# One core, gated cross-attention and feed-forward products: a frozen order of operations in place of a list planned at build time

## The chip, the cores and the metric

The kernel runs on one core of a Trainium2 chip. The metric is the device time of one execution in microseconds (us); the median of several runs is compared. One execution of each kernel was also recorded by the hardware profiler, and "the profile", "the trace" and "the timeline" below are views of that one execution.

## The reference, cut to what matters

```python
def fake_quant(x, scale, zp):
    q = jnp.clip(jnp.round(x / scale + zp), 0.0, 255.0)
    return (q - zp) * scale

x = x + tanh(g_xattn) * (fake_quant(layernorm(x)) @ fake_quant(ctx_4096))     # (2,1024,2048) @ (2,2048,2048)
x_ei = concat([layernorm(x)[..., :1638], -4.0 * layernorm(x)[..., 1638:]])
x = x + tanh(g_ffn) * scale * einsum('bsi,if->bsf', x_ei, kernel)            # kernel: 2048 x 2048, boolean
```

Both products have 2048 rows of tokens (two batches of 1024), an inner length of 2048 and 2048 output columns. The first product works on whole numbers from 0 to 255, the second on 32-bit floats against a matrix of zeros and ones.

## The kernel before

**Stages.** Tokens are cut into 16 tiles of 128 rows, eight for each batch; two tiles make a pair, and two pairs a quarter `q`. For batch 0 the order is: normalise and quantise the x tiles (`ops_norm1`), quantise the context columns chunk by chunk (`ops_kv`, four chunks `c` of 512 columns, eight loads `g` of 512 KB each), multiply (`mm1`, line 544), add the result to x (`add_row1`, `add_out1`, lines 592 and 596, both on POOL), take the second statistics (`stats`, line 426), scale (`scale2`, line 685), turn by TensorE (`turn2`, line 692), split into a high and a low part (`part_hi`, line 738, ACT; `part_lo`, line 742, DVE or POOL), and multiply with the weights widened from bytes (`widen`, line 782, ACT; `mm2`, line 809). The second product is done for pairs of tiles as seven half-size products `M1` to `M7` with sums of blocks (`combine`, lines 722 to 728, DVE or POOL; `combine_w` for the weights, line 767, DVE); results are added by `add2` (line 825, DVE) onto rows that `load_back` fetched. Batch 1 follows; half of its first product is done in seven products too (`mm1s`, line 646).

**The start.** `load_x` and `load_kv` (lines 420 and 518) are all issued by SP's one queue. `fill_kv` (line 522) is a POOL memset that clears a page before quantised context bytes are written into it. A tile's `stats` (DVE), `variance` (DVE, lines 431 and 433), `square_root` (ACT, line 438) and `factor` (DVE, eight small instructions from line 447) come before its `quant1` (ACT line 470 or DVE line 472), `turn1` (TensorE, line 503) and `take1` (ACT line 512 or DVE line 514). `quant_kv` (ACT line 530 or DVE line 532) quantises one load of context. `sums_mm` (line 556) are TensorE's column sums of the first context chunks, two matmuls for each call; `sums_pair` (lines 565 and 568) prepare those of later chunks on DVE; `row1` (ACT, line 578) takes the column sum. `rowsum1` (ACT line 478, or DVE line 480) sums a token's bytes, and `out1` (ACT line 586 or DVE line 588) takes a product out of PSUM.

**Who sets the order.** Every step is recorded by `op(engines, f, ...)` with the engines that may do it, its reads, writes and buffers. `Plan.order` then plays the recorded steps through a table of durations and waits written in the kernel, 80 times with shifted due times, and returns the best list found, with an engine for every step that has a choice. The list is walked once, and each step emits its instructions:

```python
for o in order:
    if len(o.engines) > 1:
        o.f(*o.args, engine=o.engine)
    else:
        o.f(*o.args)
```

The place of a step in the list therefore fixes three things: its place in its engine's queue (each engine works strictly in order), which of the 44 pages or of the PSUM buffers it gets, and whose release that buffer waits for. A DMA also waits for the landing of the eighth DMA ahead of it.

Of the kernel before, what the change touches and what calls it, by code (L numbers as in the profile page):

```python
# [20 lines left out]
P = 128  # L21
# [5 lines left out]
PAGES = 44  # L27


class Op:  # L30
    __slots__ = ("engines", "f", "args", "deps", "users", "due", "lead", "opens", "uses",
                 "place", "end", "left", "index", "engine", "bias", "port", "ready")


class Plan:

    def __init__(self, buffers):
        self.free = dict(buffers)
        self.ops = []
        self.place = 0.0
        self.writer = {}  # L50
        self.readers = {}
        self.opener = {}
        self.kind = {}
        self.count = {}
        self.first = None

    def op(self, engines, f, *args, reads=(), writes=(), opens=(), main=False, due=None, lead=80, bias=0.0,
           port=False, in_turn=False):

        o = Op()
        o.engines, o.f, o.args, o.lead, o.index = engines, f, args, lead, len(self.ops)
        o.deps, o.users, o.uses, o.opens = set(), [], set(), []
        o.place, o.ready = None, 0.0
        o.due, o.bias, o.port = due, bias, port
        for kind, buf in opens:
            assert buf not in self.opener, buf
            self.opener[buf], self.kind[buf], self.count[buf] = o, kind, 0
            o.opens.append(buf)  # L70
        for key in reads:
            if key in self.writer:
                o.deps.add(self.writer[key])
            self.readers.setdefault(key, []).append(o)
            o.uses.add(key[0])
        for key in writes:
            if key in self.writer:
                o.deps.add(self.writer[key])
            o.deps.update(self.readers.pop(key, ()))
            self.writer[key] = o  # L80
            o.uses.add(key[0])
        for buf in o.uses:
            if buf in self.opener:
                o.deps.add(self.opener[buf])
                self.count[buf] += 1
        if in_turn:
            if self.first is not None:
                o.deps.add(self.first)
            self.first = o
        o.deps.discard(o)  # L90
        for d in o.deps:
            d.users.append(o)
        if main:
            o.place = self.place
            self.place += min(engines.values())
            o.due = o.place if due is None else due
        self.ops.append(o)
        return o

    def dues(self):  # L100
        inf = float("inf")
        given = [o.due for o in self.ops]
        for o in reversed(self.ops):
            d = inf if o.due is None else o.due
            for u in o.users:
                if u.place is not None or u.due is not None and u.due < inf:
                    d = min(d, (u.due if u.place is None else u.place) - min(o.engines.values()) - 3)
            o.due = d
        for o, g in zip(self.ops, given):
            if o.due == inf:  # L110
                o.due = max([d.due for d in o.deps] + [0.0]) + 50

    def order(self, lag, start, runs, seed=1):


        self.dues()
        chance = random.Random(seed)
        free, count = dict(self.free), dict(self.count)
        dues = [o.due for o in self.ops]
        best = None  # L120
        for i in range(runs):
            self.free, self.count = dict(free), dict(count)
            try:
                end = self.run(lag, start)
            except RuntimeError:
                end = None
            if end is not None and (best is None or end <= best[0]):
                best = end, self.began, [o.engine for _, _, o in self.began]
                dues = [o.due for o in self.ops]
                held = self.held_up()  # L130
            for o, due in zip(self.ops, dues):
                o.due = due
            for ops in held:
                if chance.random() < 0.5:
                    step = chance.choice((3.0, 6.0, 12.0, 24.0))
                    for o in ops:
                        o.due -= step
            if i % 3:
                place = chance.uniform(0.0, self.place)
                for o in self.ops:  # L140
                    if o.place is None and abs(o.due - place) < 120.0 and chance.random() < 0.1:
                        o.due += chance.uniform(-25.0, 25.0)
        _, self.began, engines = best
        for (_, _, o), e in zip(self.began, engines):
            o.engine = e
        return [o for _, _, o in self.began]

    def held_up(self):

        before, begin, all_ = {}, {}, []  # L150
        for s, _, o in self.began:
            begin[o] = s
            last = before.get(o.engine)
            before[o.engine], before[o] = o, last
            if o.place is None or last is None or s - begin[last] - last.engines["PE"] < 1.0:
                continue
            ops = []
            x = o
            for _ in range(8):
                x = self.rel.get(x)  # L160
                if x is None or x.place is not None:
                    break
                ops.append(x)
                p = before.get(x)
                if p is not None and begin[p] + p.engines[p.engine] > x.ready + 1.0:
                    break
            all_.append(ops)
        return all_

    def run(self, lag, start):  # L170


        self.rel = {}
        ready = {}
        events = []
        began = []
        for o in self.ops:
            o.left = len(o.deps)
            o.end = 0.0
        tick = 0  # L180

        def push(time, what, o):
            nonlocal tick
            tick += 1
            heappush(events, (time, tick, what, o))

        for o in self.ops:
            if not o.left:
                for e in o.engines:
                    push(0.0, "ready", (e, o))  # L190
        done = set()
        engines = sorted({e for o in self.ops for e in o.engines}, key=lambda e: (e != "PE", e))
        for e in engines:
            ready[e] = []
        busy = {e: e in start for e in engines}
        for e, time in start.items():
            push(time, "idle", e)
        port = 0.0
        progress = 0.0
        now = 0.0  # L200
        idle = 0.0
        last_pe = 0.0
        while len(began) < len(self.ops):
            if not events:
                self.began = began
                raise RuntimeError("the plan is stuck")
            now, _, what, o = heappop(events)
            if what == "ready":
                e, o = o
                if o not in done:  # L210
                    heappush(ready[e], (o.due + o.bias, o.index, o))
            elif what == "idle":
                busy[o] = False
            else:
                for buf in o.uses:
                    if buf in self.count:
                        self.count[buf] -= 1
                        if not self.count[buf]:
                            self.free[self.kind[buf]] += 1
                for u in o.users:  # L220
                    u.left -= 1
                    u.end = max(u.end, now)
                    if not u.left:
                        self.rel[u], u.ready = o, now
                        for e in u.engines:
                            wait = 0.0 if e == o.engine and e != "SP" else lag.get((o.engine, e), lag[e])
                            push(now + wait, "ready", (e, u))
            if events and events[0][0] <= now:
                continue
            again = True  # L230
            while again:
                again = False
                for e in engines:
                    if busy[e]:
                        continue
                    held = []
                    found = None
                    while ready[e]:
# [991 lines left out]
```

## Time and profile before

| what | value |
|---|---|
| median of 3 runs | 698.88 us (698.78 to 699.11) |
| the profiled execution: span, first to last instruction | 697.0 us |
| TensorE (PE): busy, matmuls | 674.0 us, 3180 |
| DVE, ACT, POOL: busy | 490.2, 455.4, 316.8 us |
| first matmul starts | 13.23 us |
| last matmul instruction starts | 692.2 us |
| granted TensorE clock, mean | 1.000 |

The profiled execution has no time of its own beside its span: the page gives 697.0 us, and the median of the timed runs lies 1.9 us above it. In the profile's rows, an arrow `out<-in` names the tiles that an instruction writes and reads; "idle before" is the time for which the engine did nothing just ahead of an instruction, with what ended it.

### The profile page before, as it was taken

To read this page: it belongs to the slowest core of one execution; us is meant where nothing else is said; L and a number is where in the kernel's file an instruction comes from. 1 tells how busy PE (TensorE), PEld (TensorE's weight loads), DVE (VectorE), ACT (ScalarE), POOL (GpSimd) and SP (SyncE) were. 2 spreads that over 40 slices of the span, in tenths; PEclk is the share of its full clock that TensorE was granted. 3 is DMA by queue.
4 is the path that set the end of the run, shared out by engine and by line. 5 is a ranking of instruction groups with operands and counts; after the bars stand their busy time and mean duration, and the time that the engine had idled before them with its cause. 6 is when DMAs were issued, how large, how long until landed. Compare 5 with 4: busy or idle time off the path is not lost.

```text
span 697.0 us, 8833 instructions
## 1 busy us (share of the span) xinstructions
PE 674.0 (97%) x3180; PEld 471.7 (68%) x3180; DVE 490.2 (70%) x717; ACT 455.4 (65%) x536; POOL 316.8 (45%) x210
## 2 busy tenths in 40 slices
PE   1999999989999999999999999999999999999997
PEld 0444444468788888878885444447888888888885
DVE  6899958899998886497878888468572425583331
ACT  4599444286888566699926768229699347689540
POOL 8166789863625221855717887975120101040000
PEclk9999999999999999999999999999999999999999
DMA  8999406777995799477379677327074379155032
GB/s 302 393 393 380 162 13 231 259 261 251 361 400 225 233 324 339 140 247 278 120 263 330 222 268 245 121 92 275 27 260 162 105 231 324 67 170 222 22 131 90
DMA packets 63580, 155.78 MB, mean 223 GB/s; under 512 B 4912, under 2 KB 21296, under 8 KB 63536
## 3 DMA queue, kind: packets, MB, share of 16 engines
q1 hardware_dynamic: 63536, 155.21, 62.9%
q8 instruction: 25, 0.41, 0.2%
q14 instruction: 19, 0.16, 0.1%
HBM read 117.44 MB, written 37.75 MB: 223 GB/s over the span
## 4 chain that ended last, share of the span: by engine, by line
PE 87%; DMA 4%; DVE 4%; POOL 2%; ACT 2%; issue 1%; SPq 0%; ACTq 0%; DVEq 0%
PE acc_M L809 57%; PE acc L544 19%; PE acc_M L646 7%; PE tr L692 4%; DMA kv<-in_kv_dram 3%; DMA x<-in_x_dram 1%; POOL x L596 1%; DVE wB L767 1%; ACT wf_M L782 1%; POOL x L592 1%; PE tr L503 1%; DVE qn L472 0%; PE cs L574 0%; DVE x L685 0%; DVE bn_b L426 0%
## 5 line engine op out<-in xcount | busy, mean ns | idle before, releaser
L809 PE MATMUL acc_M<-wf_M,hi_M 128*128 128x512 f32 x896 | 282.0, 395 | 1.6 <-ACT wf_M L782 1.5
L809 PE MATMUL acc_M<-wf_M,lo_M 128*128 128x512 f32 x896 | 277.6, 390 | 0.6 <-POOL lo_M L742 0.6
L782 ACT ACTIVATE wf_M<-wr_M 128x1024 fp32r<-128x1024 uint8 x224 | 221.6, 1050 | 26.8 <-DMA wr_M<-in_wmask_dram 24.2
L809 PEld LDWEIGHTS acc_M<-wf_M,lo_M 128*128 128x128 f32 x896 | 168.0, 188 | 36.8 <-POOL lo_M L742 1.3
L809 PEld LDWEIGHTS acc_M<-wf_M,hi_M 128*128 128x128 f32 x896 | 164.1, 188 | 34.4 <-ACT wf_M L782 3.2
L544 PE MATMUL acc<-q,q1T 128*128 128x512 f16 x768 | 171.6, 381 | 1.2 <-DVE q1T L514 0.8
L825 DVE SCALAR_TENSOR_TENSOR back<-acc_M,f,back 128x1024 f32<-128x1024 f32 (+1 forms) x58 | 72.1, 1245 | 124.7 <-PE acc_M L809 117.1
L742 POOL TENSOR_TENSOR lo_M<-A,hi_M 128x1024 fp32r<-128x1024 f32 x24 | 62.1, 2586 | 179.5 <-ACT hi_M L738 160.1
L544 PEld LDWEIGHTS <-q1T 128*128 128x128 f16 x768 | 75.2, 98 | 90.2 <-issue 1.9
L592 POOL TENSOR_TENSOR x<-x,row 128x512 f32<-128x512 f32 x64 | 88.6, 1408 | 43.8 <-ACT sd_a L438 15.5
L596 POOL TENSOR_TENSOR x<-x,e 128x512 f32<-128x512 f32 x64 | 92.0, 1458 | 30.6 <-ACT e L586 16.1
L738 ACT CAST hi_M<-A 128x1024 fp32r<-128x1024 f32 x48 | 50.1, 1044 | 13.1 <-POOL A L726 4.7
L530 ACT ACTIVATE q<-kv,sc,rs 128x1024 uint8<-128x1024 f32 x45 | 53.5, 1236 | 7.8 <-DMA kv<-in_kv_dram 5.1
L586 ACT ACTIVATE e<-acc,tokb,f1u 128x512 f32<-128x512 f32 x34 | 25.1, 774 | 49.6 <-PE acc L544 47.8
L426 DVE BATCH_NORM_STATS2 bn_b<-x 128x6 f32<-128x512 f32 x64 | 43.1, 684 | 15.9 <-POOL x L596 15.6
L495 ACT COPY A<-tr 128x512 f32<-128x512 f32 x35 | 20.3, 584 | 46.5 <-PE tr L692 45.8
L742 DVE TENSOR_TENSOR lo_M<-A,hi_M 128x1024 fp32r<-128x1024 f32 x24 | 33.7, 1421 | 7.2 <-ACT hi_M L738 7.2
L568 DVE TENSOR_TENSOR pair<-pair,q 128x1024 f16<-128x1024 f16 x36 | 36.6, 1022 | 2.5 <-ACT q L530 0.8
L728 POOL TENSOR_TENSOR A<-A,A 128x1024 f32<-128x1024 f32 x8 | 21.1, 2648 | 23.7 <-DVE A L726 16.4
L522 POOL MEMSET q<- 128x1024 f32 x32 | 29.2, 952 | 5.1 <-DVE q L532 2.2
L512 ACT ACTIVATE q1T<-tr 128x1024 f16<-128x1024 uint8 x22 | 21.3, 1019 | 7.5 <-PE tr L503 6.8
L767 DVE SCALAR_TENSOR_TENSOR wB<-wB,wB 128x2048 uint16<-128x2048 uint16 x8 | 24.2, 3031 | 0.0
(103 smaller groups left out, 594.1 us busy)
## 6 DMA issues: line engine op xcount, KB each, us to landing
kv<-in_kv_dram SPq DMA_DIRECT2D x64, 512.0 KB, 9.2
x<-in_x_dram SPq DMA_DIRECT2D x32, 512.0 KB, 7.7
x<-x SPq DMA_DIRECT2D x32, 512.0 KB, 3.0
back<-x SPq DMA_DIRECT2D x32, 512.0 KB, 6.1
wr_M<-wt_T SPq DMA_DIRECT2D x32, 512.0 KB, 5.6
out_dram<-back SPq DMA_DIRECT2D x30, 512.0 KB, 3.6
wr_M<-in_wmask_dram SPq DMA_DIRECT2D x24, 512.0 KB, 5.4
n<-in_x_dram SPq DMA_DIRECT2D x16, 512.0 KB, 7.2
```

What stands on the lines that cost most here:

```text
L426: nc.vector.bn_stats(bn[v, t][:, c, :], xt[src[v, t, c // 2]][:, ts(c % 2, NB)])
L530: nc.scalar.activation(low, v, AF.Identity, bias=z2, scale=rs2)
L544: nc.tensor.matmul(acc1[b, c, tiles[0]][:, i, :], q1T[tiles[i]][:, k, :], rhs1(b, c, k), start=(k == 0), stop=(k == KT - 1),)
L568: nc.vector.tensor_add(colsum[b, c], colsum[b, c], v[:, i : i + 2, :])
L592: nc.gpsimd.tensor_add(xc, xc, colrow[b, c])
L596: nc.gpsimd.tensor_add(xc, xc, ev.pop((t, c)))
L646: nc.tensor.matmul(acc1[key][:, i, :], left_half(p, LEFT1[m])[:, 4 * s + k, :], right1(m, h, s)[:, k, :], start=(m in OPENS and s == 0 and ...
L738: nc.scalar.copy(hi[m, p], A[left(m, p)])
L742: engines[engine].tensor_sub(lo[m, p], A[left(m, p)], hi[m, p].bitcast(F32))
L782: nc.scalar.activation(wf[q, m, k], wr[q, m, k // 4][:, k % 4, :], AF.Copy, bias=-float(RIGHT[m][1]))
L809: nc.tensor.matmul(acc2[SUM[m], p][j], part[m, p][:, k, :], wf[q, m, k][:, ts(j, NB)], start=(m in OPENS and k == 0 and part is hi), stop= ...
L825: nc.vector.scalar_tensor_tensor(v, acc, f2, v, ALU.mult, ALU.add)
```

## The change

`Plan` loses its durations, its search and its queue model. `op` still records steps, reads, writes and buffers, and ignores all hints. A string of 2314 words takes the place of the list: a word is a step's number, with D, A or P (DVE, ACT, POOL) where a step has a choice of engine.

```diff
-    order = plan.order({("ACT", "SP"): 8.0, ("POOL", "SP"): 12.0, ("DVE", "SP"): 12.0, "PE": 6.0, ... }, {"SP": 13.0, "DVE": 22.0, "ACT": 22.0}, 80, 2)
-    for o in order:
-        if len(o.engines) > 1:
-            o.f(*o.args, engine=o.engine)
-        else:
-            o.f(*o.args)
+    plan.run(ORDER_OF_OPS)
...
+    def run(self, order):
+        names = {"D": "DVE", "A": "ACT", "P": "POOL"}
+        done = set()
+        for word in order.split():
+            o = self.ops[int(word.rstrip("DAP"))]
+            assert o not in done and o.deps <= done
+            done.add(o)
+            if len(o.engines) > 1:
+                o.f(*o.args, engine=names[word[-1]])
+            else:
+                o.f(*o.args)
+        assert len(done) == len(self.ops)
...
+ORDER_OF_OPS = """
+17 1 137 0 35 38 16 40 95 42 32 48 90 100 37 21 33 20 45 85 5 4 43 84 2 143 3 50 36D 149 6 58 7 19 155 8 213 59
+41A 207 18 9A 47 44D 201 22 94 34A 10D 23 87 229 39A 195 24 11 231 12A 53 233 235 46D 25A 237 89 220 221 13A 26D
...
```

All 2314 steps are the same ones. What differs is their place on each of the five engines, and the engine of 150 of the 342 steps with a choice. The first steps of each queue show the kind of difference (tiles as `load_x(tile, half)`, context as `load_kv(batch, chunk, g)`; `stats(tile, chunk)`):

| queue | before | after |
|---|---|---|
| SP | x(0,0) x(0,1) x(1,0) x(1,1) kv 0,1,2,3,4,5,6,7 | x(1,1) x(0,1) x(0,0) kv 1, x(1,0), kv 3,4,0,2,5, kv(0,1,0), kv 7, x(3,0) x(3,1), kv 6 |
| POOL | 16 fills, in the order of their use | the same 16 fills in another order |
| DVE | stats of tile 0, variance 0, stats(1,0) stats(1,1), factor 0, stats(1,2) stats(1,3), variance 1, quant_kv 1, factor 1 | stats(1,3) (1,2) (0,3) (0,2) (0,0) (0,1), quant_kv 1, variance 0, stats(1,1), factor 0, stats(1,0), quant_kv 4, variance 1, quant1(0,1), factor 1 |
| ACT | sqrt 0, quant_kv 0, quant1(0,0), quant1(0,1), sqrt 1, quant_kv 2, 3, take1(0,0), take1(0,1) | sqrt 0, quant_kv 3, quant1(0,0), quant_kv 0, sqrt 1, quant_kv 2, take1(0,0), quant1(1,0), take1(0,1) |
| PE | sums_mm, turn1 0, 3 sums_mm, 3 mm1 of tile 0, turn1 1 | sums_mm, turn1 0, 4 sums_mm, 4 mm1 of tile 0, turn1 1 |

Further on, the first `turn2` of the second product stands near the end of chunk 0's product of tiles 6 and 7, in place of the start of chunk 3's. Ahead of the first `mm2` stand seven `widen` (four before), two `part_lo` (one before) and three `combine_w` (five before).

## The prediction

> **What bounds it now.** I read the page's head and slices first, then the list of PE's waits, the chain of waits from 120 to 200 us, and the timelines of the start. The head and the slices:
>
> ```profile
> span 697.0 us, 8833 instructions
> PE 674.0 (97%) x3180; PEld 471.7 (68%) x3180; DVE 490.2 (70%) x717; ACT 455.4 (65%) x536; POOL 316.8 (45%) x210
> ...
> PE   1999999989999999999999999999999999999997
> ```
>
> PE is the bound all the way; only the first slice and one about 145 us are not full. Every matmul stays in the change, so time can come only out of PE's gaps. In PE's list of waits:
>
> ```profile
> PE cs L556 <- ACT q L530: 13.2, 1, 13.2
> PE acc_M L809 <- ACT wf_M L782: 1.5, 2, 1.4
> ```
>
> Only the first wait is large. I took the starts of successive matmuls from the trace: 216 ns apart on lines 544, 556 and 646, 227 ns on 809, 109 ns for transposes; what exceeds this is a gap. All matmuls at these paces, with 0.087 us at each of 49 changes from `turn2` to line 809, are 670.9 us of solid work. The gaps are: 13.2 us to the first matmul; half pace (427 ns) until 21.3 us; 2.4 us between 30 and 45 us; 4.0 us after that (0.73 + 0.11 at 145, 1.53 + 0.11 at 151, 0.32 at 186, 0.57 at 258, 0.19 at 299, 0.46 at 394). The last matmul starts at 692.2, the rest is the last add and store, the same in both lists.
>
> The 2.4 us at 145 to 152 come from DVE, by the chain of waits:
>
> ```profile
> 140.39 1.23 DVE wB L767
> ...
> 146.45 3.30 DVE wB L767
> 149.75 0.74 DVE A L706 x2
> ...
> 151.52 1.06 ACT wf_M L782
> ...
> 152.62 8.50 PE acc_M L809 x36
> ```
>
> Weight sums (`combine_w`) stand between DVE's steps for the first `mm2`. The start is the part that decides; timelines of ACT, DVE, POOL and PE:
>
> ```profile
> 11.94 1.24 ACT L530 ACTIVATE q<-kv,sc,rs 128x1024 uint8<-128x1024 f32 x1 [2.03 <-DMA kv<-in_kv_dram]
> 12.33 3.62 POOL L522 MEMSET q<- 128x1024 f32 x4
> 14.23 2.27 DVE L532 TENSOR_SCALAR q<-kv,rs,sc 128x1024 uint8<-128x1024 f32 x1
> 13.23 1.01 PE L556 MATMUL cs<-q,ones_h 128*128 128x512 f16 x2 [13.23 <-ACT q L530]
> 16.55 2.72 PE L556 MATMUL cs<-q,ones_h 128*128 128x512 f16 x6 [0.36 <-DVE r_a L447]
> ```
>
> `quant_kv` on DVE, 0.81 us at its median, took 2.27: it was asked for inside the 15th fill (over at 15.06) and ended at 16.49, which is 0.54 after the 16th and last fill (15.95). It did not get in between two fills. The same against one more fill:
>
> ```profile
> 293.27 2.42 POOL L726 TENSOR_TENSOR A<-A,A 128x1024 f32<-128x1024 f32 x1
> 295.61 0.96 POOL L522 MEMSET q<- 128x1024 f32 x1
> 293.94 3.19 DVE L532 TENSOR_SCALAR q<-kv,rs,sc 128x1024 uint8<-128x1024 f32 x1
> ```
>
> It waited past the end of line 726 (295.69) and ended 0.55 after the fill (296.58). Against two POOL additions it did get in:
>
> ```profile
> 141.48 4.42 POOL L742 TENSOR_TENSOR lo_M<-A,hi_M 128x1024 fp32r<-128x1024 f32 x1
> 145.86 5.03 POOL L596 TENSOR_TENSOR x<-x,e 128x512 f32<-128x512 f32 x2
> 144.79 1.66 DVE L685 TENSOR_SCALAR x<-x,mv_b,r_b 128x1024 f32<-128x1024 f32 x1
> ```
>
> `scale2` ended at 146.45, 0.55 after line 742's end (145.90), and the addition begun at 145.86 had to wait.
>
> **The change, part by part.** It adds and removes no operation.
>
> *The first matmul.* Loads of 512 KB land 1.34 us apart: the first is used at 6.59, the fifth at 11.94. In the new order of SP's queue kv 1 is fourth (10.6), x(1,0) fifth (11.9), kv 3 sixth (13.3), kv 0 eighth (16.0). On DVE the six `stats` of the first three loads fill the time to 10.6; then comes `quant_kv` 1, ahead of `variance` 0, and POOL's 16 fills run from 1.68 to 15.95 as before, since they wait for nothing. This is the unknown of the sum: how long that `quant_kv` waits. Bounds: it gets in after the fill under way (ends 11.2, as `scale2` did between additions), or after the last fill (ends 16.5, as the same instruction did in two of two cases against fills). I take the second, because those two rows are the same pair of instructions.
>
> From 16.5: `variance` 0.45, `sqrt` 0.25, `stats`(1,1) 0.65 beside it, `factor` 1.83: 19.4. On ACT `quant_kv` 3 stands behind `sqrt` and is done by then; `quant1`(0,0) 1.2 and `quant_kv` 0 1.2 end at 21.8. The first matmul needs that one: 21.8 against 13.23. If the wait ends at 11.2: `sqrt` 11.9, `stats` 12.6, `factor` 14.4, `quant1` 15.7, kv 0 lands at 16.0, first matmul 17.25.
>
> Before, PE could not use its early start: by 21.5 us it had done 14 matmuls and 4 transposes, 3.46 us of full-pace work, so it was 18.05 behind a solid start at zero. After, PE has its work in hand from the first matmul on; with the 4.8 us at half pace that followed 16.55 before, 2.4 are lost. Behind: 21.8 + 2.4 = 24.2, or 17.25 + 2.4 = 19.65. The start costs 6.15 us, or 1.6.
>
> *20 to 45 us.* From the column sum of chunk 0 to `take1`(2,0), ACT has in the new order 2 `row1`/`sqrt` 0.7, 2 `out1` 1.36, 2 `quant1` 2.26, 5 `quant_kv` 5.65, 2 `take1` 1.8, `rowsum1` 2.03: 13.8 us by the rows' spacing. PE has 50 matmuls, 2 `turn1` and a `rowsum1_pe` there, 12.06. So 1.8 us of gaps, in place of 2.4: a gain of 0.6 and a price of 5.55 (or 1.0) by 45 us.
>
> *45 us to the end.* `turn2`, `part_lo` and `widen` of the first `mm2` stand earlier and two `combine_w` later, so the gaps at 145 to 152 go; I let all 4.0 us go, and 0.3 for three fewer changes from `turn2` to line 809. What is late next, I looked for by adding rows on one engine between a PE release and PE's next need, in the new order. Three places have under 0.4 us to spare. About 188 us DVE has `add2`, `combine`, `stats`, `combine_w` and `part_lo`, 7.3 us between two PE needs, with 3.2 for `combine_w`, whose rows run from 2.28 to 3.91: 0 to 1.5 us, taken 0.5. About 339 us ACT's `widen` waits for pages that POOL frees with `part_lo` and two `combine` (2.4 each, up to 4.4 where DVE is in the way): 0.2 to 2.7, taken 1.5. Some ten other places have 0.4 to 1 us: 0 to 2, taken 0.5. Together 0.2 to 6.2, taken 2.5.
>
> *The sum.* 697.0 + 5.55 - 4.0 - 0.3 + 2.5 = 700.75 of span; timed runs lie 1.9 above the span: **702.7 us**, with 700.4 to 706.4 by the bounds of the last term.
>
> A rule to weigh: the Trainium skill, page "SBUF — State Buffer", section "SBUF: two separate sides", says that whichever of the two engines starts first holds the shared pair for its whole instruction, while the other blocks. By it alone `quant_kv` would wait for one fill, and the sum would be the first rival's. The row at 14.23 us speaks against so short a wait.
>
> **Rivals.** *DVE gets in between two fills.* Span 697.0 + 1.0 - 4.0 - 0.3 + 2.5 = 696.2, or 698.1 us timed, 695.8 to 701.8. It is faster than before by more than can be told from no change (0.2%, 1.4 us) where the new gaps after 45 us stay below 1.9 us. For it: `scale2` at 144.79. Against: the fills run with 0.06 us of overlap, and the instruction lost at both handovers to a fill.
>
> *Transfers come too late.* Many loads stand only 2.7 us of PE work ahead of their first user in the new list, as `load_back` of the last pair's M4 does; before, most stand over 6 us ahead, and landings take 5.4 to 6.1 us from issue at the median. Where SP cannot run ahead of the list, DVE or ACT waits up to 3.4 us each time, behind it the next `part_lo`: one or two such on top of the forecast give 707 or more. Against: in the trace SP issues `load_back` 4.9 us ahead of its place at the median.
>
> That the list is the old one is excluded: none of the five queues stands in the same order.
>
> **How the numbers follow.** DVE shut out to the last fill 0.52, all slower. DVE in between fills 0.43: spread over 695.8 to 701.8, 0.25 faster, 0.13 within 0.2%, 0.05 slower. Late transfers 0.05, slower. So faster 0.25, same 0.13, slower 0.62. The range takes the rival's time less its lower bound to the forecast's upper one: 696 to 706; the likeliest case's own is 700.4 to 706.4.
>
> **What would show it.** Right: `quant_kv` on DVE from about 10.6 to 16.5 us, first matmul near 21.8, no gap at 145 to 152 us. Wrong: that row at 0.8 to 1.5 us and a first matmul near 17; or new gaps above 3 us after 45 us.

## The result, and the profile after

| | before | after |
|---|---|---|
| median of the timed runs | 698.86 us (698.78 to 699.11, 4 runs) | 711.95 us (709.46 to 712.12, 4 runs) |
| the profiled execution: span | 697.0 us | 710.4 us (timed 712.12 us) |
| first matmul; PE behind solid work at 49 us; the same at the last matmul | 13.23; 20.5; 25.0 us | 21.64; 25.7; 38.4 us |

The ratio is 1.0179, with a 95% interval from 1.0164 to 1.0194: the new table is slower by 13.1 us. The sign was forecast, the size was not: 702.7 us, with a range up to 706. In kernel.py of after each line stands 97 lower than before (the widen of line 782 is now 685, the store of 829 is 732). "Behind solid work" is the start of a matmul less all PE work ahead of it at the paces of the prediction, but with a change from `turn2` to `mm2` at 0.01 us in place of 0.087 (the part on why the prediction was right or wrong says from which rows). The head of the page, and its row of slices:

```profile
span 710.4 us, 8767 instructions
PE 675.6 (95%) x3180; PEld 471.6 (66%) x3180; DVE 489.1 (69%) x749; ACT 433.1 (61%) x500; POOL 328.0 (46%) x213
PE   0799999999998999999999999999999999999997
```

PE's busy time is 1.6 us longer; the first slice is now empty and the notch has moved from the 9th slice to the 13th, at 213 to 231 us. The list of PE's own waits (line waited for: total, times, longest):

```profile
PE cs L459 <- ACT q L433: 21.6, 1, 21.6
PE acc_M L712 <- ACT wf_M L685: 4.2, 4, 1.9
...
PE cs L477 <- DVE pair L471: 0.8, 1, 0.8
PE acc_M L712 <- ACT hi_M L641: 0.8, 1, 0.8
PE acc_M L712 <- DVE back L728: 0.7, 1, 0.7
PE tr L595 <- ACT A L607: 0.5, 1, 0.5
```

Before, the waits for `widen` were two, 1.5 us together. The timelines of the start show the forecast row:

```profile
1.67 14.27 POOL L425 MEMSET q<- 128x1024 f32 x16
10.68 5.81 DVE L435 TENSOR_SCALAR q<-kv,rs,sc 128x1024 uint8<-128x1024 f32 x1
21.64 1.01 PE L459 MATMUL cs<-q,ones_h 128*128 128x512 f16 x2 [21.64 <-ACT q L433]
```

`quant_kv` 1 asked at 10.68 and ended 0.55 after the last fill. The new gaps lie later. I list all above 0.15 us after 49 us, as excess over a matmul's pace: 0.19 at 150 us, 0.85 at 184, 0.35 at 190, 0.40 at 194, 0.95 at 205, 2.09 at 217 with 1.6 of half pace behind it, 1.02 at 283, 0.35 at 338, 0.60 at 351, 0.19 at 367, 1.25 at 375, 0.19 at 378, 0.95 at 447, 0.69 at 494: 11.7 us. The timeline ahead of the largest, SP, POOL, ACT and PE together:

```profile
200.55 0.42 SPq L732 DMA_DIRECT2D out_dram<-back  x1
205.47 1.03 ACT L641 CAST hi_M<-A 128x1024 fp32r<-128x1024 f32 x1
209.43 2.40 POOL L645 TENSOR_TENSOR lo_M<-A,hi_M 128x1024 fp32r<-128x1024 f32 x1 [5.36 <-DMA out_dram<-back]
211.78 4.77 POOL L631 TENSOR_TENSOR A<-A,A 128x1024 f32<-128x1024 f32 x2
216.58 3.90 ACT L685 ACTIVATE wf_M<-wr_M 128x1024 fp32r<-128x1024 uint8 x4 [0.80 <-POOL A L631]
219.59 0.89 PE L712 MATMUL acc_M<-wf_M,hi_M 128*128 128x512 f32 x2 [1.93 <-ACT wf_M L685]
```

Read from the bottom: PE waits for a `widen`, this one for a page that two `combine` read, these stand behind a `part_lo`, and that `part_lo` waited for a page that still belonged to a store, issued at 200.55 and landed at 209.3. POOL was idle for 5.36 us ahead of it; the other input, ACT's `part_hi`, was ready at 206.5, so the store accounts for the last 2.9 us. The chain of waits around 375 us has the same kind in fewer steps:

```profile
363.55 1.29 DVE back L728
...
364.87 8.28 DMA out_dram<-back
...
373.21 2.96 ACT wf_M L685 x3
...
376.22 1.21 PE acc_M L712 x4
```

A store takes 8.28 us to land, then `widen` gets its page, and PE waits. Followed back in this way, the gap at 184 goes to DVE's `stats` of a batch-1 load (issued 170.9, landed 183.5) queued ahead of an `add2`; 190 to a weight load (178.5 to 187.3); 205 in part to a store of summed weights (187.2 to 195.8); 283 to a weight load behind three stores (271.5 to 281.1). From 150 to 180 us the DMAs of after took 8.3 us from issue to landing on average and 12.6 at most (20 of them), those of before 5.3 and 7.3 (17). The DMA share does not explain it (0.80 in after, 0.88 in before, over these 30 us). What differs is how many were on their way at once: 20 x 8.3 / 30 = 5.5 on average, against 17 x 5.3 / 30 = 3.0.

Late landings alone make no gap, however. From 185 to 226 us the DMAs of before took 7.0 us on average and 10.4 at most, and from 360 to 376 us 7.8 and 10.8, as long as those of after (7.1 and 9.5; 7.1 and 9.1), and PE had no gap above 0.32 us there. That points to the order: it leaves less time between a transfer and the work that needs its page or its data (in the prediction's count many loads stand 2.7 us of PE work ahead of their first user, against over 6 before). Its stores of the output also land later: 5.0 us on average and 10.2 at most (34 stores), against 3.8 and 5.6 before.

### The profile page after: what moved, and what is told of

Same layout as the page of the kernel before. It is cut to its first block, busy times and chain, and to the rows that moved or that the text cites. A ratio compares the mean times of both kernels' runs of the same rounds, so it can differ in the third digit from the quotient of the medians.

```text
span 710.4 us, 8767 instructions
## 1 busy us (share of the span) xinstructions
PE 675.6 (95%) x3180; PEld 471.6 (66%) x3180; DVE 489.1 (69%) x749; ACT 433.1 (61%) x500; POOL 328.0 (46%) x213
## 4 chain that ended last, share of the span: by engine, by line
PE 47%; DVE 4%; DMA 3%; ACT 2%; POOL 2%; issue 1%; SPq 0%; ACTq 0%; POOLq 0%; DVEq 0%
PE acc_M L712 37%; PE acc L447 4%; PE acc_M L549 3%; PE tr L595 2%; DVE pair L471 2%; DMA out_dram<-back 1%; ACT wf_M L685 1%; DMA kv<-in_kv_dram 1%; DVE bn_b L329 1%; DMA x<-in_x_dram 1%; POOL A L631 1%; DVE q L435 1%; ACT q L433 1%; POOL x L499 0%; POOL lo_M L645 0%
## 5 line engine op out<-in xcount | busy, mean ns | idle before, releaser
L499 POOL TENSOR_TENSOR x<-x,e 128x512 f32<-128x512 f32 x64 | 96.0, 1514 | 47.5 <-ACT e L489 26.2
L495 POOL TENSOR_TENSOR x<-x,row 128x512 f32<-128x512 f32 x64 | 94.3, 1491 | 42.8 <-ACT row L481 40.7
L645 POOL TENSOR_TENSOR lo_M<-A,hi_M 128x1024 fp32r<-128x1024 f32 x19 | 46.4, 2446 | 131.2 <-ACT hi_M L641 92.6
L645 DVE TENSOR_TENSOR lo_M<-A,hi_M 128x1024 fp32r<-128x1024 f32 x29 | 41.8, 1443 | 30.8 <-ACT hi_M L641 17.8
L433 ACT ACTIVATE q<-kv,sc,rs 128x1024 uint8<-128x1024 f32 x37 | 45.1, 1237 | 17.7 <-DMA kv<-in_kv_dram 10.0
L471 DVE TENSOR_TENSOR pair<-pair,q 128x1024 f16<-128x1024 f16 x36 | 33.8, 945 | 0.9
L435 DVE TENSOR_SCALAR q<-kv,rs,sc 128x1024 uint8<-128x1024 f32 x27 | 31.4, 1167 | 3.8 <-DMA kv<-in_kv_dram 2.3
L459 PE MATMUL cs<-q,ones_h 128*128 128x512 f16 x32 | 10.4, 432 | 21.6 <-ACT q L433 21.6
L400 DVE COPY A<-tr 128x512 f32<-128x512 f32 x23 | 15.7, 686 | 18.4 <-PE tr L595 16.3
L625 POOL TENSOR_TENSOR S<-A,A 128x1024 f32<-128x1024 f32 x6 | 16.0, 2664 | 25.8 <-issue 16.4
```

What stands on the lines that cost most here:

```text
L433: nc.scalar.activation(low, v, AF.Identity, bias=z2, scale=rs2)
L435: nc.vector.tensor_scalar(low, v, rs2, z2, ALU.mult, ALU.add)
L471: nc.vector.tensor_add(colsum[b, c], colsum[b, c], v[:, i : i + 2, :])
L495: nc.gpsimd.tensor_add(xc, xc, colrow[b, c])
L499: nc.gpsimd.tensor_add(xc, xc, ev.pop((t, c)))
L645: engines[engine].tensor_sub(lo[m, p], A[left(m, p)], hi[m, p].bitcast(F32))
```

## The experiments

Two theories for the 11.7 us: *transfers* land late in full stretches and hold up DVE, ACT and POOL; or *engines*, the new places and engine letters giving DVE, ACT and POOL too much between two needs of PE. Kernels e1 to e4 have their line numbers 18 higher than after. Gaps are read from one execution of each kernel; the four timed runs of after itself lie between 709.46 and 712.12 us. The runs of before beside them had medians of 698.74 to 698.80 us.

**e1, the start by DVE's order.** One word moved:

```diff
-3 50 36D 149 6 58 7 19 155 8 213
+3 50 149 6 58 7 19 155 8 36D 213
```

> One word of the new table is moved: quant_kv 1 of chunk 0 on DVE (36D) stands behind factor 0, no longer ahead of variance 0. Theory (the quant was shut out by POOL's fills from 10.68 to 16.49 us, and variance, sqrt and factor stood behind it): variance starts near 10.7, factor ends near 14, quant1(0,0) near 15.3, and the first matmul then waits for kv 0, which lands at 16.0, and its quant: 17.3 us in place of 21.6. The time falls by 4.3 less what kv 1's quant makes late, to 707.5 to 708.5 from 711.95. Rival (the start is set by the loads' order, kv 0 eighth on SP's queue, and by ACT's list): first matmul stays above 20, time 711 to 712.

710.64 us (1.0170, 1.0156 to 1.0184). The first matmul came at 17.28 and PE was 21.2 behind at 49 us, as expected; but only 1.3 us of it were left at the end. PE met new gaps of 0.37 at 60 and 1.26 at 87 us, this one waiting for DVE's sums of pairs (`pair` alone, no transfer), and new or larger ones at 279 (1.50), 321 (0.51) and 356 (1.09).

**e11, the start by POOL's fills.** DVE's order is untouched:

```diff
-fill_kv(0,2,1) (0,2,2) (0,2,3) (0,3,3) (0,3,2) (0,3,1) (0,3,0) among the first 54 words
+the first two behind add_row1(0,0,1), the others behind add_row1(0,0,0)
```

> The new table with seven of POOL's 16 fills (six of chunks 2 and 3 plus one) moved behind the first two add_row1, so that POOL is free from about 9.7 us; DVE's order is that of the new table. Lockout: quant_kv 1 on DVE takes 0.8 to 0.9 us from 10.7 in place of 5.81, variance 0 starts near 11.5, and the first matmul is at 17.3 (kv 0 lands at 16.0 and takes 1.2), as with the quant moved. The time then is that of the moved quant, 710 to 711, if the start's gain is given back in the same way. Rival (quant_kv 1 was slow for another reason, its transfer or its page): the row stays over 4 us.

```profile
1.68 8.06 POOL L425 MEMSET q<- 128x1024 f32 x9
...
10.12 0.82 DVE L435 TENSOR_SCALAR q<-kv,rs,sc 128x1024 uint8<-128x1024 f32 x1
```

These are timelines of POOL and DVE. With POOL idle the same instruction at the same place in DVE's queue took 0.82 us in place of 5.81, and the first matmul came at 17.02. That settles the lockout. The time was 710.93 us (1.0192, 1.0161 to 1.0223): most of the gain of the start is given back, as in e1. (The profiled execution took 716.54 us, with two stretches at half clock later on.)

**e3 and e4, start and rest exchanged.**

```diff
-plan.run(words of the new table)
+e3: first 210 words of the old list, then the other words in the new order
+e4: first 210 words of the new table, then the other words in the old order
```

> A table with the first 210 words of the old list (to about 49 us of work), then all other words in the new order. If start and rest add up: the start's 5.2 us go (offset of the matmuls at 49 us 25.67 after against 20.47 before), the new gaps after 49 us stay (about 11 us, against 4.0 in the old order): 711.95 - 5.2 = 706.8. If the gaps after 49 us are a consequence of the late start (loads issued by a queue that runs ahead, PE late against it), they shrink and the time is below 703.

> The counterpart: the first 210 words of the new table, then all other words in the old order. If start and rest add up: 698.9 + 5.2 = 704.1, first matmul at 21.6, gaps at 145 to 152 us (2.4 us of the old order) still there, no gap of over 0.6 us between 180 and 220. If the rest suffers from the late start, 706 or more.

e4: 703.81 us (1.0070, 1.0057 to 1.0084), 5.0 above before: in the old order the late start costs all that was forecast, and no new gap over 0.35 us followed between 158 and 220 us. e3: 714.18 us (1.0221, 1.0207 to 1.0235), worse than after, which neither theory expected. The splice itself made gaps of 3.5 and 2.0 us at 58 to 64 us, where PE waited to turn a tile that the old start had not prepared, with half pace behind them (6.8 us of half clock); so its total says nothing of the start. Past 150 us its gaps stand at the places of after (1.31 at 208, 1.52 at 220, 1.21 at 284, 1.67 at 377): they belong to the list, not to the late start.

**e2 and e6, SP's queue alone.**

```diff
-e2: store2(1,0,0) (685) behind load_x(9,1)
+e2: 685 behind add2(M6,0) (713)
-e6: 1156 ... 1182 1188 1151 720 ... 721 ... 701 ... 559 ... 685 ... 1316 ... 949
+e6: 1151 1156 ... 720 1182 ... 721 1188 ... 559 701 ... 684 685 ... 949 1316
```

> One word of the new table is moved: the store of the result of M6 (store2(1,0,0), SP) stands right behind its add2, 30 words earlier and ahead of load_w(M4,0) and two loads of batch 1, in place of behind them. Theory of transfers (PE's gap of 2.1 us at 217 us goes back through a widen, two combines on POOL and a part_lo on POOL that waited 5.4 us for the page of this store, which was issued at 200.6 and landed at 209.3): the store is issued near 196, the part_lo starts near 204 to 205, the gap at 217 goes and with it the half pace until 223 us, 3.8 us together: 708.2. If only the gap goes, 709.9. Theory of engines (the gap comes from the two combines of 2.4 us and from ACT's list of widen and quant1, which stand where they stood): the gap stays above 1.5 us, time 711 to 712.

> The new table with six words of SP's queue at other places and no word of another engine moved: load_x(8,1) ahead of load_x(9,0); load_w(M7,0) ahead of load_x(10,0); load_x(11,0) behind load_w(M7,1); store_t(1,0) ahead of load_back(1,0,1); the store of tile 2's first half right behind its last add2; load_w(1,M1,1) ahead of two loads of context. Theory of transfers: each lands some 3 to 8 us earlier for the instruction that waited on it, and the gaps at 184 (0.85), 190 (0.35), 205 (0.95), 217 (2.1, with half pace 3.8) and 283 us (1.0) shrink to under a third: 706 to 708. Theory of engines: gaps within 0.5 us of those of after, 711 to 712.

The store of e2 holds the results up to `add2(M1,1)`, not of M6 as the expectation says, and could have gone earlier still; e6 puts it there. e2: 712.22 us (1.0196, 1.0182 to 1.0210), no faster than after. The store landed at 202.3, and the `part_lo` behind it started at 207.96 in place of 209.43, now waiting for ACT's `part_hi`. The gap at 217 fell to 1.06 without half pace, which is what neither theory said, but 0.47 more came at 184, 0.68 at 225 and 0.46 at 375, and the half clock of the start lasted until 27.48 in place of 25.46 us in this execution, 1.0 us of loss. A single move freed one wait and showed the next. e6: 709.14 us (1.0149, 1.0136 to 1.0162), 2.8 below after with nothing but SP's queue changed: 190 and 283 gone, 217 down to 0.36; but 184 (0.80), 205 (1.12) and 375 (1.34) stayed, and a new one of 1.91 at 223 followed an `add2` behind `stats` that waited for another load. The 0.95 at 447 was missing too, which SP's queue does not account for (see e5). This speaks for transfers, at about half of the expected gain or less.

**e5 and e9, shorter stores.**

```diff
 def store2(p, i, h, js=(0, 1)):
     t, a, z = 2 * p + i, js[0] * NB, (js[-1] + 1) * NB
+    z = a + (z - a) // 8
```

> The new table, with the final stores of the output writing one eighth of their columns (64 KB in place of 512 KB; the rest of the output is left out). No instruction and no place is changed, only the transfers are shorter. Theory of transfers (in the trace of after, PE's gaps at 217, 283 and 375 us go back to a page whose store landed 8.3 to 8.7 us after its issue, or to a weight load queued behind three stores): these gaps (2.1 with 1.7 of half pace, 1.0, 1.25) go, the ones at 184, 190 and 205 us stay, and the time is 706 to 708 in place of 711.95. Theory of engines (DVE, ACT and POOL have too much to do between two needs of PE): the gaps stay within 0.5 us, time 711 to 712.

> Control for the short stores: the kernel before, with the final stores writing one eighth of their columns (the rest of the output is left out). If late transfers are a loss of the new order alone: none of the gaps of before (145, 151, 186, 258, 394 us) was traced to a landing, so 698.8 less at most 0.7, which the shorter last store may take off the end. If shorter stores help any order: 695 or less.

e5: 704.63 us (1.0083, 1.0071 to 1.0095), 7.3 below after and more than expected. The gaps at 205, 217, 283 and 375 are under 0.25, 184 is 0.29, and 447 is gone; left are some 4.2 us in all, with a new gap of 0.66 at 222. PE's waits from 50 us on, and POOL's timeline at the place of the largest gap:

```profile
PE tr L595 <- ACT A L607: 0.8, 1, 0.8
PE acc_M L712 <- DVE back L728: 0.5, 1, 0.5
PE acc_M L712 <- ACT wf_M L685: 0.3, 1, 0.3
```

```profile
205.84 2.40 POOL L645 TENSOR_TENSOR lo_M<-A,hi_M 128x1024 fp32r<-128x1024 f32 x1 [2.92 <-DMA out_dram<-back]
208.19 4.76 POOL L631 TENSOR_TENSOR A<-A,A 128x1024 f32<-128x1024 f32 x2
```

The `part_lo` starts 3.6 us earlier, the two `combine` take what they took, and nothing waits for them. No instruction was moved, so engine work is the same. From 360 to 376 us the DMA share fell from 0.98 to 0.73. Shorter stores let go of their pages earlier and also let the loads behind them pass, so e5 alone does not part the two; the traces of after put 217 and 375 down to a held page, 283 to a load behind stores.

Two of the gaps that shrank are not the stores' doing. At 184 (0.56 less) no store of the output has been issued yet; this gap is 0.45 to 1.45 in e1, e2, e3, e11 and e12, which have DVE's order of after there. At 447 (0.95 less) PE waits for DVE's sums of pairs: a row takes 0.70 us alone and 1.65 beside POOL's additions, and by a small shift in time two rows more or fewer fall beside them. The gap is in e1, e11 and e12 (short stores), and not in e2, e3, e6 and e15 (stores as they were). e9, the control: 697.72 us (0.9985, 0.9976 to 0.9994), 1.06 below before, a little more than the 0.7 expected; the last matmul started at 692.14 us against 692.18, so nearly all of it is the shorter last store. The old order loses nothing that shows to stores. The new one loses some 5 to 6 us: 7.3 less 1.06 for the last store, less part or all of the 1.5 us at 184 and 447.

**e12, both.** The moved word of e1 and the short stores of e5.

> The moved quant_kv 1 and the short stores together (output left out as before). With the stores as they are, the moved quant gained 4.3 us at the first matmul and 4.5 by 49 us, of which 1.3 were left at the end: 1.6 were given back at 60 and 87 us, before any store of the output, and the rest at 279 to 356 us. If the give-back behind 270 us is late transfers: short stores keep it out, 704.6 - 2.7 = 701.9. If it is DVE, ACT or POOL being late against an earlier PE: 703.3 or more.

703.17 us (1.0062, 1.0049 to 1.0076), 1.5 below e5, between the two expectations. In the profile the gain of the start was given back in gaps of 2.4 us before 90 us (1.26 of it DVE's sums of pairs), a larger one at 184 (1.45), and 0.95 at 440 us, the sums of pairs again. At 279 to 356 us, where e1 gave back, no gap is above those of e5: what e1 lost there goes with late transfers, and the other part was lost earlier, to DVE and to the late load at 184.

**e15, DVE's order at 184 us.**

```diff
-1185 ... 1153 1155 ... 600D
+600D 1185 1153 1155
```

> The new table with three stats of batch 1 on DVE (tile 10 chunk 1, tile 8 chunks 1 and 3) moved behind take2(3,1,1), behind add2(M1,0), with all loads where they were. If the gap at 184 us is add2 queued behind a stats that waits for a load landing at 183.5: it goes (0.85, 0.80 to 1.45 in the other runs of this order), while the gaps at 205, 217, 283 and 375 us stay: 710.5 to 711.5. If PE's gap at 184 has another setter, it stays above 0.6.

711.54 us (1.0188, 1.0173 to 1.0204). The gap at 184 went, so it was the `add2` behind the late load; but 1.25 us came at 188 to 189 and the gap at 205 grew to 2.28. The matmul behind the gap at 205 came at 207.48 us, against 206.49 in after: ACT began the work ahead of it behind the same landing (195.8 us in both, a store of summed weights), but had six `widen` to do there in place of five. In e5 that store landed at 194.6.

**e7 and e8, the engine letters exchanged.**

```diff
-plan.run(words of the new table)
+e7: the new order of steps, each with its letter of the old list
+e8: the old order of steps, each with its letter of the new table
```

> The new order of the words, with the engine letters of the old list for the 150 steps where the two differ (25 take2 from DVE to ACT, part_lo and combine exchanged between DVE and POOL, and so on). If the choice of engine makes the new gaps: they shrink and the time is below 706. If places in the queues and transfers make them: the letters were chosen for their own places, so others in these places do no better, and the time is 712 or more.

> The old order of the words with the engine letters of the new table. If the letters make the loss: 705 or more, with gaps after 150 us. If the order makes it: within 3 us of the 698.8 of before, unless the letters fit the old places badly, which gaps at places of their own would show.

732.30 us (1.0483, 1.0469 to 1.0496) and 714.68 us (1.0230, 1.0216 to 1.0244). Letters fit their own places only. e8 lost 3.6 us at one place alone (449 us, where PE waited for sums of pairs). These two do not tell the theories apart.

**e10, e13, e14, e16, e17: are the old gaps free to take?** All on the old list, each with the edits of those ahead of it:

```diff
+e10: combine_w(0,2) (550) behind part_lo(M2,1); combine_w(1,1) (560) behind factor of tile 7; their stores 551, 561 later
+e13: also stats(8,0..2) (1152, 1153, 1154) behind add2(M1,1)
+e14: also combine_w(1,3) (564) behind add2(M1,0), its store 565 behind load_w(M7,0)
+e16: also combine(0,2) 626P -> 626D
+e17: also combine(0,1) 625P -> 625D
```

> The old list as a table, with two combine_w on DVE moved out of the way of the first mm2: combine_w(0,2) behind part_lo(M2,1), combine_w(1,1) behind factor of tile 7, and their store_t behind store_t(0,1) and load_b(B21,1). If the gaps at 145 (0.73) and 151 us (1.5) come from these weight sums, as the prediction said: both go, 696.6 to 697.0. If the moved sums make a transfer late (store_t, load_w), a new gap between 155 and 220 us takes some of it back: 697 to 700.

> The old list with the two combine_w moved as in the run before it (their gaps at 145 and 151 us went, but 2.4 us came back at 179 to 186, because from 170 us on DVE ran at the very times of before), and with three stats of tile 8 moved from 171 us behind add2(M1,1) at 184 us, 1.8 us of DVE's work between 163 and 182 us. If DVE's total work up to 182 us is what sets PE's place at 182: the gap at 179 (1.48 and 0.30) shrinks to under 0.3, and the time is 696.9 to 697.3. If the gap has another setter (POOL's combine of 2.4 and 4.3 us, or a transfer): 698.5 to 699.

> The same, and combine_w(1,3) (3.0 us, at 173 us) moved behind add2(M1,0) with its store_t behind load_w(M7,0). If DVE is the setter: the next 0.3 to 0.6 us go too, 696.5. If the late store_t makes a weight load late, a new gap of over 1 us appears between 190 and 230 us: 698 or more.

> The order of the run with two sums later (698.27 us; its gaps at 179 and 180 us, 1.5 together, wait for POOL's part_lo at 178.4, behind POOL's combine of 3.26 and 2.40), with combine(0,2) on DVE in place of POOL. If POOL's combine is the setter: part_lo starts near 176.5, the two gaps go, 696.8 to 697.2. If DVE then is late with combine(1,1), (1,2) for the place at 186 us: a gap there of 1 us or more, 698.

> The same with combine(0,1) on DVE too: both at 1.2 us, from 171.3, in place of 2.4 and 3.3 on POOL. If POOL is the setter: part_lo near 175, no gap at 180 and none over 0.3 at 186, 696.7. If DVE has no room: gaps of 1 us or more between 180 and 195, 698.

| run | us | ratio | gaps between 140 and 190 us, without those under 0.2 |
|---|---|---|---|
| before | 698.8 | | 0.73 and 1.44 at 145 and 151; 0.32 at 186 |
| e10 | 698.90 | 1.0002 (0.9993 to 1.0011) | 1.48, 0.30, 0.60 at 179 to 186 |
| e13 | 700.16 | 1.0017 (1.0009 to 1.0026) | 2.23, 0.28 at 179 to 182, then half pace (1.4) |
| e14 | 698.27 | 0.9992 (0.9983 to 1.0001) | 0.37, 1.14, 0.24 at 179 to 186 |
| e16 | 697.95 | 0.9988 (0.9979 to 0.9997) | 1.30 at 184 |
| e17 | 696.63 | 0.9970 (0.9959 to 0.9981) | none |

In e10 the gaps at 145 and 151 were gone, and PE's 2.4 us came back at 179 to 186, since from 170 us on DVE and POOL ran at the times of before to within 0.1 us. My reading that DVE's total work sets that place fell with e13: less DVE work there made it later. The setter was POOL, whose `combine` ahead of a `part_lo` is drawn out when DVE works beside it, as POOL's timeline of e10 shows:

```profile
171.66 2.41 POOL L627 TENSOR_TENSOR A<-A,A 128x1024 f32<-128x1024 f32 x1 [3.52 <-DVE S L625]
174.14 4.33 POOL L629 TENSOR_TENSOR A<-A,A 128x1024 f32<-128x1024 f32 x1
179.64 2.37 POOL L645 TENSOR_TENSOR lo_M<-A,hi_M 128x1024 fp32r<-128x1024 f32 x1 [1.17 <-ACT hi_M L641]
```

The `part_lo` waits there for ACT's `part_hi` of the sum, and this for the `combine`. With both on DVE (e17, timelines of DVE and POOL) it starts 4.2 us earlier than in e10, and 3.0 earlier than in e14 (178.44):

```profile
171.70 1.22 DVE L627 TENSOR_TENSOR A<-A,A 128x1024 f32<-128x1024 f32 x1
173.02 1.22 DVE L629 TENSOR_TENSOR A<-A,A 128x1024 f32<-128x1024 f32 x1
...
175.41 2.41 POOL L645 TENSOR_TENSOR lo_M<-A,hi_M 128x1024 fp32r<-128x1024 f32 x1 [7.09 <-ACT hi_M L641]
```

e17 is faster than both kernels, by 0.3% against before.

## Why the prediction was right or wrong

**The start: right.** The row, its end against the last fill, the first matmul (21.64 for 21.8) and the price by 45 us (5.2 for 5.55) came as worked out; e11 shows the lockout by taking POOL away. The rule weighed there, from the Trainium skill, page "SBUF — State Buffer", section "SBUF: two separate sides", was read as a wait for the one fill under way. The section says it of a DVE instruction in a two-port mode (or with two inputs in SBUF, against a GpSimd instruction that reads SBUF), and does not say who wins when one fill ends and the next begins. Here DVE asked at 10.68, inside a fill, and lost five handovers in a row, to the fills that began at 11.44, 12.33, 13.22, 14.10 and 14.99; the measurement decides against that reading. What the sum could not say is that the price and the rest do not add: the late start costs 5.0 us in the old order (e4), and taking it away gained only 1.0 to 1.3 in the new (e1, e11), where an earlier PE ran into DVE's sums of pairs at 87 us and into late transfers.

**The 4.0 us of old gaps: right.** In after 0.19 us at 150 is left. That they go when `combine_w` moves is right for e10 too; that they stay away needs the next late chain to be shorter as well.

**The three fewer changes, 0.3 us: misread.** In the trace of before the first `mm2` matmul behind a `turn2` starts 28 ns after the last transpose (their pace is 109), and the next one 314 ns after it (pace 227). The prediction counted the second as a loss of 87 ns and not the first as a gain of 81, so a change costs 0.01 us and three are worth 0.03. Solid work is then 667.2 us and not 670.9; with 670.9 the gaps that the prediction lists overshoot the last matmul's start (670.9 + 18.05 + 2.4 + 4.0 = 695.4, against 692.2). The forecast rests on differences, so it moves by 0.3 us alone.

**The new gaps after 45 us: the step that failed.** The sum had 2.5 us, with 6.2 at most; the trace has 11.7. They were looked for "by adding rows on one engine between a PE release and PE's next need". For gaps of this sort that was near: 0.40 at 194 (taken 0.5), 0.95 at 338 and 351 (taken 1.5), and 2.2 at 150, 367, 378, 447 and 494 (taken 0.5), 3.6 in all, inside the bounds. What it left out are the 8.1 us at 184, 190, 205, 217, 283 and 375 us, which begin with a landing. They are the rival "Transfers come too late", given 0.05; its price, 707 or more, was of the right order. It was put aside with medians: landings of "5.4 to 6.1 us", and SP issuing a load 4.9 us ahead of its place "at the median". The six landings behind these gaps took 8.3 to 12.6 us. And it spoke of loads alone: the two most expensive gaps come from stores, which hold a page until they have landed, a release that the description of the kernel names for every buffer, and that no row of the sum had. Of the 8.1 us, the 6.9 at 205, 217, 283 and 375 went with shorter stores (e5 against e9), the 0.35 at 190 with SP's order alone (e6), and the 0.85 at 184 when DVE's wait for the late load was moved (e15).

With the measured terms the sum is 697.0 + 5.2 - 4.0 + 11.7 = 709.9, against a span of 710.4. Not settled: how much of the gap at 205 is transfer and how much ACT's own queue. It went with the short stores (e5), but in e15 it grew with no transfer moved. Nor do the runs say how much the engine letters do in their own places: e7 and e8 put them in places that they were not chosen for.

## What to carry to other kernels

When a frozen order is judged, follow the page releases as well as the loads: a store's landing can free the page that POOL, ACT and then TensorE wait for, and the two that cost most here landed 8.3 and 8.7 us after their issue, about twice the stores' median of 4.5. Take landing times from the stretch where they matter, and their tail, and hold them against the time that the order leaves; the old order had landings as late in places and lost nothing by them. A stall taken out at one place is won only if the next chain to the same engine is shorter too; look for it before counting the gain, and try the engine that has room.

## What the runs showed of the hardware that I had not expected

TensorE's clock can fall after a gap of little more than 2 us. Windows of after (us, busy times, granted clock as the third value from the end):

```profile
217.00:219.60 2.60, 0.67 (x4) 0.21 (x3) 2.53 (x8) 2.60 (x4) 0.00 (x0) 1.00 0.96 356
219.60:223.00 3.40, 3.40 (x9) 2.67 (x10) 3.01 (x10) 3.40 (x4) 0.00 (x0) 0.56 1.03 393
```

Behind the gap of 2.09 us the clock record has 0.5 for 3.41 us, and matmuls start 0.43 us apart: 1.6 us more, for a wait of 2.09. The same 3.41 us at half followed gaps of 2.23 us (e13) and 2.75 us (e11), and two of 0.88 and 1.60 us with 0.9 us of work between them (e11), but not those of 2.28 (e15) and 1.91 us (e6). The Trainium skill, page "TensorE: Matmul & The Clock Gate", section "What's actually happening", tells of a free-running window of 3413 ns, which fits the length and the element of chance; the rule of its section "HAM oscillation — how this bites in real kernels", no idle gaps above about 3.4 us, is too generous for this kernel, where 2.1 us were enough.
